# First attention, first block: written order, rows normed a step ahead, row loads on ScalarE's queue

## The chip, the cores and the metric

The kernel runs on one core of a Trainium2 chip. The metric is the device time of one execution in microseconds, as the median of several runs. The engines of the core work side by side, each through its own list of instructions: TensorE (PE in the profile, with PEld for its weight loads) multiplies matrices into PSUM, VectorE (DVE) and ScalarE (ACT) do elementwise work, GpSimd (POOL) does the rest, and SyncE (SP) issues transfers. ScalarE can issue transfers as well.

## The reference

N = 2708 rows of width 256 and an adjacency matrix of N x N go through two layers, each an attention over the graph and a mixture of eight experts. The change lies in the first layer's attention:

```
xn = layernorm(x)                       # per row, no weights
q, k, v = xn @ Wq.T + bq, xn @ Wk.T + bk, xn @ Wv.T + bv
scores = where(adj > 0, q @ k.T / 16, -9e15)
x = x + elu(softmax(scores) @ v)
x = x + experts0(layernorm(x))          # top 2 of 8, gelu
x = x + graph attention of layer 1 (layernorm(x))
x = x + experts1(layernorm(x))
```

## The kernel before

`layer0_attention` handles the queries in six blocks (`BLOCKS`): five of 512 rows and one of 148. For each block it walks over 22 key tiles of 128 rows (`k`, the last has 20 rows). The projections of queries and keys are folded into one matrix `aT`, so that the keys of a tile are simply the normed rows, transposed: `xnT`.

A key step `k` of block `b` does the following. `scores` multiplies `xnT` of the tile with the block's queries `g` (L578), takes the exponential on ScalarE (L590) and multiplies by the mask on VectorE (L593). `attend`, three steps later (`LAG`), multiplies the masked `p` with the values `v` and adds up in four banks of PSUM (L642). In the profile each score step has four matmul records and each attend step eight.

In block 0 the key tiles have to be prepared too, tile `k + 4` in step `k`. `norm_begin` takes statistics on VectorE (L274 to L276) and a power on GpSimd (L280). `norm_end` norms the row tile on VectorE (L284). `prepare` then transposes it on TensorE (`to_columns`, L297), copies the result from PSUM to `xnT` on ScalarE (L298), sums it on VectorE (L491), multiplies it with `wv` on TensorE (L496) and copies the values out on ScalarE (L500). The rows themselves come through `load_x` (L400), nine tiles ahead, into nine buffers (`xin`).

Also in block 0, `masks_of` turns adjacency rows into masks on VectorE (a comparison L438 and a transpose L444): the generator `first_mask` for block 0 and `later_mask` for block 1. Both load through SyncE (L417, four transfers for one buffer) and share three buffers (`adj`).

SyncE issues in written order in the whole kernel. For the other engines a planner orders the instructions by readiness and estimated costs, unless they stand in a region of `manual_schedule`: in such a region each engine that it names issues in the order in which the code emits. Before the change such a region for TensorE, ScalarE and VectorE begins with block 1 and goes on to the end of the first experts; block 0 is the planner's. A smaller region for VectorE and GpSimd covers the norming of tiles 0 to 3 and the first masks. Tiles 0 to 3 are prepared, and the queries of block 0 computed, ahead of the loop.

Of the kernel before, what the change touches and what calls it, by code (L numbers as in the profile page):

```python
# [27 lines left out]
NT = (N + P - 1) // P  # L28
ROWS = [min(P, N - t * P) for t in range(NT)]
# [14 lines left out]
def of_tile(rows, t):  # L44

    if t >= KEYS:
        return rows[t * P : t * P + ROWS[t], :]
    b = t // GROUP * BN
    return rows[b : b + BN, :].rearrange("(p j) d -> j p d", j=GROUP)[t % GROUP]
# [57 lines left out]
def adj_ffn_kernel(ctx: ExitStack, tc: tile.TileContext, a: dict, out: bass.AP):  # L107
    nc = tc.nc
# [267 lines left out]
    def layer0_attention(line):  # L376
        with ExitStack() as scope, ExitStack() as until_last:
# [17 lines left out]
                return pool.tile(shape, dtype, name=f"{name}_last", bufs=bufs)  # L395
            xin = {}

            def load_x(t):
                xin[t] = rows0.tile([P, D], F32, name="xin", bufs=9)
                nc.sync.dma_start(xin[t][: ROWS[t]], of_tile(a["x"], t))  # L400

            def masks_of(b, of):

# [68 lines left out]
            def norm_begin(t):  # L472
                r, src = ROWS[t], xin.pop(t)
                return t, src, norm_stats(src[:r], r)

            def norm_end(t, src, stats):
                r, (mean, factor, *_) = ROWS[t], stats
                xn = rows.tile([P, D], F32, name="xn", bufs=4)
                normed(xn[:r], src[:r], mean, factor)
                return xn  # L480

            def prepare(t, xn):
                r = ROWS[t]
                at = xnT[:, :, t * P : t * P + r]
                if t < NT - 1:
                    to_columns(at, xn[:r], r)
                else:
                    tail_columns(x_tail, xn)
                    nc.vector.tensor_copy(at, x_tail[:, :, :r])
                    r, at = P, x_tail  # L490
                nc.vector.tensor_reduce(  # L491
                    sums_of[:, :, t], xnT[:, :, t * P : t * P + ROWS[t]], AX.X, ALU.add
                )
                ps = misc.tile([P, GROUP, P], F32, name="misc").rearrange("p g n -> p (g n)")
                for c in range(DC):
                    nc.tensor.matmul(  # L496
                        ps[:r, :D], at[:, c, :], wv[:, c, :],
                        start=(c == 0), stop=(c == DC - 1),
                    )
                nc.scalar.copy(v[:r, t, :D], ps[:r, :D])  # L500
# [3 lines left out]
            if True:  # L504
# [8 lines left out]
                with tc.manual_schedule(  # L513
                    engines={mybir.EngineType.DVE, mybir.EngineType.Pool}
                ):
                    begun = [norm_begin(t) for t in range(2)]
# [39 lines left out]
            def queries(b):  # L556
                b0, nb, _ = BLOCKS[b]
                g = of_block(b, "g", [P, DC, nb], F32)
                for d in range(DC):
                    ps = misc.tile([P, GROUP, P], F32, name="misc").rearrange("p g n -> p (g n)")  # L560
                    for c in range(DC):
                        nc.tensor.matmul(
                            ps[:, :nb], aT[:, c, d * P : (d + 1) * P], xnT[:, c, b0 : b0 + nb],
                            start=(c == 0), stop=(c == DC - 1),
                        )
                    nc.scalar.activation(
                        g[:, d, :nb], ps[:, :nb], AF.Identity, bias=cq[:, d : d + 1]
                    )
                return g
# [103 lines left out]
            for t in range(4):  # L673
                prepare(t, first[t])
            g = queries(0)
            late, total, accs, apart = [], None, None, None
            folding = fold_gate(wide)
            for b, (b0, nb, ts_) in enumerate(BLOCKS):
                line.gap = GROUP if b >= last - 1 else GROUP + 1
                if b == 1:  # L680
                    order0.enter_context(
                        tc.manual_schedule(engines={
                            mybir.EngineType.PE,
                            mybir.EngineType.Activation,
                            mybir.EngineType.DVE,
                        })
                    )
                if b + 1 < len(BLOCKS):
                    turned_of[b + 1] = mask_of(b + 1)
                if b == 0:  # L690
                    later_mask = masks_of(1, turned_of)
                    next(later_mask)
                for k in range(NT):
                    if b == 0:
                        if k + 9 < NT:
                            load_x(k + 9)
                        next(first_mask, None)
                        if k + 4 < NT:
                            prepare(k + 4, norm_end(*norm_begin(k + 4)))

                    j = k - (2 if b == last else NT - 1 - GROUP)
                    if 0 <= j < len(ts_):
                        load_x(ts_[j])
                    if k == (0 if b == last else GROUP):
                        apart_adj = load_apart(b)
                    if k == NT - 8:
                        apart = compare_apart(*apart_adj)
                    late.append((b, k, scores(b, k, g, apart, mT)))
                    if len(late) > LAG:
                        b_, k_, p = late.pop(0)  # L710
                        if k_ == 0:
                            accs = [
                                ps_acc.tile([P, D + 1], F32, name="acc") for _ in BLOCKS[b_][2]
                            ]
                        attend(b_, k_, p, accs)
                        if k_ == NT - 1:
                            evict(b_, accs, total)
                    if b == 1 and k % 2 == 0:
                        next(folding, None)
                    if b == 0 and k == NT - 1:  # L720
                        sums = wide.tile([P, DC], F32, name="sums", bufs=1)
                        nc.vector.tensor_reduce(sums, sums_of, AX.X, ALU.add)
                        total = all_sum(wide, sums, wv, D, "total0")
                    if b == 0 and k == NT - 4:
                        raw = wide.tile([P, BN // QUARTER, P], I32, name="adj", bufs=3)
                        raw = raw.rearrange("p n e -> p (n e)").bitcast(F32)
                        nc.sync.dma_start(
                            raw, a["L0_ffn_Wr"].rearrange("d e -> (d e)").partition_broadcast(P)
                        )
                        gate_rows(raw)  # L730
                    if k == NT - 6 and b + 1 < len(BLOCKS):
                        g_next = queries(b + 1)
                    if k % 3 == 2 if b == last - 1 else k == 0 or k >= 2:
                        next(later_mask, None)
                    if k == NT - 3:
                        even_later = iter(())
                        if b + 2 < len(BLOCKS):
                            even_later = masks_of(b + 2, turned_of)
                            next(even_later)
                    if b > 0 and k == 2:  # L740
                        nc.sync.dma_start(neighbours[b - 1][:], turned_of[b - 1])
                    if background and k % 2 == 1 and b < last and (b > 0 or k > 8):
                        background.pop(0)()
                    if b > 0:
                        line.step()
                    if b == last and k == LAG:
                        until_last.close()
                    if b == last and k == LAG + 2:
                        n = FULL_AFTER[experts0.early]
                        guess0 = experts0.open(  # L750
                            [i * (n // RING) * E // (n + GROUP) for i in range(AHEAD)] + [-1]
                        )
                        for _ in range(AHEAD):
                            next(guess0)
                        begin0 = experts0.begin()
                    if b == last and LAG + 2 <= k < LAG + 8:
                        next(begin0)
                    if b == last and k in (LAG + 9, LAG + 13, LAG + 18):
                        next(begin0)
                if b == last:  # L760
                    nc.sync.dma_start(neighbours[b][:], mT)
                else:
                    for _ in later_mask:
                        pass
                    later_mask = even_later
                    g, mT = g_next, turned_of[b + 1]
# [1332 lines left out]
```

## Time and profile before

| what | value |
|---|---|
| median of 3 runs | 1183.81 us (1181.85, 1183.81, 1185.64) |
| profiled execution | 1189.22 us, span of its instructions 1187.4 us |
| granted TensorE clock, mean | 0.985 |
| PE busy | 1128.9 us, 95% of the span |
| DVE busy | 649.2 us, 55% |
| ACT busy | 433.0 us, 36% |
| POOL busy | 410.2 us, 35% |
| moved by DMA | 195.88 MB, mean 165 GB/s |

Busy times are shares of the whole span, while the stages have different limits, so they have to be read stage by stage. A timeline row gives the start in microseconds, the duration, the engine, the line of the code, the operation with its output and inputs, the number of instructions that were merged into the row, and in brackets the idle time of the engine before the row, with what ended it. PE's durations overlap, because matmuls are pipelined; the pace is the distance from start to start.

### The profile page before, as it was taken

Reading aid. Unit: us, or ns where it says so; the run is one execution under the profiler, and the core shown is the slowest. Engines: PE = TensorE matmul, PEld = TensorE weight load, DVE = VectorE, ACT = ScalarE, POOL = GpSimd, SP = SyncE. Lnnn points to the kernel's source line nnn. Section 1 sums busy time; section 2 is a strip of 40 time slices with the busy share of each in tenths; the row PEclk is TensorE's granted clock in tenths of the full one; section 3 lists DMA queues with packets and bytes.
Section 4 is the critical chain, followed back from the end, with each engine's and each line's share of the span. In section 5 each row is a group of like instructions: output and inputs, shape, how many; then the busy total and the mean of one; then the engine's idle time right before and its main releaser. Section 6 shows DMA issues by size and latency. Waiting matters only on the chain. (4 is left out here: it accounts for less than half of the span.)

```text
span 1187.4 us, 20904 instructions
## 1 busy us (share of the span) xinstructions
PE 1128.9 (95%) x6417; PEld 916.1 (77%) x6417; DVE 649.2 (55%) x2401; ACT 433.0 (36%) x1260; POOL 410.2 (35%) x503
## 2 busy tenths in 40 slices
PE   8989999999999999999999999998999998879993
PEld 5665666666666675789999999996999987869992
DVE  5555777787887868552222222223866777512224
ACT  3222222222222222453333333333776758424441
POOL 3001212121212212342433343333645556435542
PEclk9999999999999999999999999999999999989997
DMA  9678677877837567478766935634001527567346
GB/s 218 134 165 207 172 173 180 229 174 200 218 83 188 142 174 267 142 209 248 199 177 189 335 73 158 178 100 107 1 1 45 207 67 222 137 209 230 82 119 237
DMA packets 200006, 195.88 MB, mean 165 GB/s; under 512 B 91004, under 2 KB 182613, under 8 KB 194377
## 3 DMA queue, kind: packets, MB, share of 16 engines
q1 hardware_dynamic: 175546, 123.97, 41.5%
q0 software_dynamic: 23872, 69.76, 18.7%
q8 instruction: 55, 0.90, 0.3%
q14 instruction: 71, 0.57, 0.2%
q10 hardware_dynamic: 462, 0.68, 0.2%
HBM read 246.19 MB, written 66.15 MB: 263 GB/s over the span
## 5 line engine op out<-in xcount | busy, mean ns | idle before, releaser
L1813 PEld LDWEIGHTS mm<-xe,ring 128*128 128x128 f32 x2192 | 262.4, 195 | 24.1 <-DVE xe L1786 8.9
L1813 PE MATMUL mm<-xe,ring 128*128 128x128 f32 x2192 | 265.2, 278 | 15.2 <-DVE xe L1786 7.9
L1821 ACT ACTIVATE hT<-mm,ring 128x128 f32<-128x128 f32 x548 | 155.6, 369 | 269.0 <-issue 177.2
L1829 PE MATMUL acc<-ring,hT 128*128 128x256 f32 x1096 | 252.8, 381 | 0.7 <-issue 0.7
L1829 PEld LDWEIGHTS acc<-ring,hT 128*128 128x128 f32 x1096 | 202.0, 191 | 25.3 <-issue 1.3
L642 PEld LDWEIGHTS acc<-v,p 128*128 128x128 f32 (+1 forms) x880 | 160.0, 190 | 62.4 <-issue 37.4
L642 PE MATMUL acc<-v,p 128*128 128x257 f32 (+1 forms) x880 | 202.7, 383 | 0.0
L578 PE MATMUL s<-g,xnT 128*128 128x512 f32 x420 | 200.3, 597 | 0.6 <-DVE mT L597 0.6
L1835 DVE SCALAR_TENSOR_TENSOR y<-acc,who,bias 128x256 f32<-128x256 f32 x92 | 44.4, 482 | 262.6 <-PE acc L1829 252.6
L1537 POOL DMA_INDIRECT disp<-row,to x88 | 91.6, 1041 | 261.6 <-DVE x L662 123.4
L280 POOL TENSOR_TENSOR ln_rs<-ln_rs,minus_half 128x2 f32<-128x2 f32 x88 | 67.7, 770 | 173.7 <-DVE ln_rs L276 121.1
L922 PE MATMUL acc<-parts,m 128*128 128x266 f32 x924 | 126.2, 293 | 0.0
L1719 POOL DMA_INDIRECT ring<-L_ffn_packed,weight_row x76 | 79.2, 1042 | 125.8 <-PE acc L1829 94.0
L922 PEld LDWEIGHTS acc<-parts,m 128*128 128x128 f32 x924 | 117.0, 185 | 4.1 <-ACT raw L949 0.9
L578 PEld LDWEIGHTS s<-g,xnT 128*128 128x128 f32 x420 | 76.8, 190 | 55.0 <-issue 49.8
L590 ACT ACTIVATE p<-s 128x512 f32<-128x512 f32 x105 | 62.3, 596 | 137.8 <-PE s L578 120.9
L1851 POOL DMA_INDIRECT xd<-y,who x45 | 71.4, 1588 | 111.3 <-DVE xe L1792 49.8
L593 DVE SCALAR_TENSOR_TENSOR p<-p,mT 128x512 f32<-128x512 f32 x100 | 70.9, 709 | 70.5 <-ACT p L590 70.4
L889 ACT CAST m<-mT 128x512 fp32r<-128x512 fp8e4 (+4 forms) x168 | 71.5, 475 | 11.1 <-PE acc L922 6.7
L1841 POOL DMA_INDIRECT xd<-y,who x47 | 50.5, 1075 | 44.5 <-DVE y L1835 34.2
L264 DVE SCALAR_TENSOR_TENSOR row<-x,wr_rows 128x256 f32<-128x256 f32 x128 | 54.3, 425 | 3.3
L1792 DVE TENSOR_SCALAR xe<-xe_raw,ring 128x128 f32<-128x128 f32 x90 | 27.2, 347 | 43.2 <-DMA ring<-L_ffn_packed,weight_row 42.2
(330 smaller groups left out, 1079.7 us busy)
## 6 DMA issues: line engine op xcount, KB each, us to landing
adj<-in_adj_dram SPq DMA_DIRECT2D x100, 256.0 KB
L_ffn_packed<-in_L_ffn_W_dram SPq DMA_DIRECT2D x32, 512.0 KB
xg<-disp SPq DMA_DIRECT2D x368, 32.0 KB
L_ffn_packed<-in_L_ffn_W_dram SPq DMA_DIRECT2D x32, 256.0 KB
neighbours<-mT SPq DMA_DIRECT2D x5, 1408.0 KB
mT<-neighbours SPq DMA_DIRECT2D x5, 1408.0 KB
ring<-L_ffn_packed SPq DMA_DIRECT2D x3, 2182.0 KB
xin<-in_x_dram SPq DMA_DIRECT2D x42, 128.0 KB
```

The costliest lines, as they stand in the source:

```text
L280: nc.gpsimd.tensor_tensor(rs[:r, 1], rs[:r, 0], minus_half[:r], ALU.pow)
L578: nc.tensor.matmul(ps[:kr, :nb], xnT[:, c, k0 : k0 + kr], g[:, c, :nb], start=(c == 0), stop=(c == DC - 1 and k < KEYS),)
L593: nc.vector.scalar_tensor_tensor(p, p, LARGEST, mask, op0=ALU.min, op1=ALU.mult)
L642: nc.tensor.matmul(accs[j][:r], p[keys, q0 : q0 + r], v[keys, k, :], start=(k == 0), stop=(k == NT - 1),)
L889: nc.scalar.copy(m[:, : q1 - q0], MASKS[b].of_key(mTs[b], k)[:, q0 - b * BN : q1 - b * BN],)
L922: nc.tensor.matmul(acc[:r], masks[t], parts[:, k, i], start=(k == 0 and i == 0), stop=False,)
L1537: nc.gpsimd.indirect_dma_start(disp[:], bass.IndirectOffsetOnAxis(ap=to[:r, j : j + 1], axis=0), rows2[:r, j], None,)
L1719: nc.gpsimd.indirect_dma_start(w, None, packed[:], bass.IndirectOffsetOnAxis(ap=self.weight_row[:, s : s + 1], axis=0), bounds_check=E * P ...
L1813: nc.tensor.matmul(ps[:, i, :], w[:, c * hidden + f * P : c * hidden + (f + 1) * P], xe[:, c, :], start=(c == 0), stop=(c == DC - 1),)
L1821: nc.scalar.activation(hT[:, f, :], ps[:, i, :], AF.Gelu, bias=w[:, b1 + f : b1 + f + 1])
L1829: nc.tensor.matmul(ps, hT[:, f, :], w[:, w2 + f * D : w2 + (f + 1) * D], start=(f == 0), stop=(f == hc - 1),)
L1851: start = nc.gpsimd.indirect_dma_start(xd[:], at, y, None, bounds_check=N - 1, oob_is_err=False, compute_op=ALU.add)
```

## The change

Block 0 is now in the region of written order as well: it begins before the loop, with the norming of tiles 4 and 5. The rows of block 0's loop are loaded from ScalarE's queue instead of SyncE's (13 loads, in steps 0 to 12). In step `k` the loop prepares tile `k + 4` from a row that was normed in the step before, norms tile `k + 5`, and begins the statistics of tile `k + 6`.

```diff
-            def load_x(t):
+            def load_x(t, queue=nc.sync):
                 xin[t] = rows0.tile([P, D], F32, name="xin", bufs=9)
-                nc.sync.dma_start(xin[t][: ROWS[t]], of_tile(a["x"], t))
+                queue.dma_start(xin[t][: ROWS[t]], of_tile(a["x"], t))
...
             for t in range(4):
                 prepare(t, first[t])
             g = queries(0)
+            order0.enter_context(
+                tc.manual_schedule(engines={
+                    mybir.EngineType.PE,
+                    mybir.EngineType.Activation,
+                    mybir.EngineType.DVE,
+                })
+            )
+            ahead = [norm_end(*norm_begin(4))]
+            begun = [norm_begin(5)]
...
             for b, (b0, nb, ts_) in enumerate(BLOCKS):
                 line.gap = GROUP if b >= last - 1 else GROUP + 1
-                if b == 1:
-                    order0.enter_context(
-                        tc.manual_schedule(engines={
-                            mybir.EngineType.PE,
-                            mybir.EngineType.Activation,
-                            mybir.EngineType.DVE,
-                        })
-                    )
...
                 for k in range(NT):
                     if b == 0:
                         if k + 9 < NT:
-                            load_x(k + 9)
+                            load_x(k + 9, nc.scalar)
                         next(first_mask, None)
                         if k + 4 < NT:
-                            prepare(k + 4, norm_end(*norm_begin(k + 4)))
+                            prepare(k + 4, ahead.pop(0))
+                        if begun:
+                            ahead.append(norm_end(*begun.pop(0)))
+                        if k + 6 < NT:
+                            begun.append(norm_begin(k + 6))
```

## The prediction

> **What bounds the kernel now.** I read the page, then the busy time by stretches, then the timeline of the first attention's first block.
>
> ```profile
> PE 1128.9 (95%) x6417; PEld 916.1 (77%) x6417; DVE 649.2 (55%) x2401; ACT 433.0 (36%) x1260; POOL 410.2 (35%) x503
> ```
> TensorE is the bound of the whole. Two stretches, the first block and blocks 1 to 4 (us, then busy time of PE, PEld, DVE, ACT, POOL, granted clock, DMA share, GB/s):
>
> ```profile
> 20.36:123.70 103.34, 96.55 (x381) 63.69 (x380) 60.08 (x174) 27.14 (x62) 9.67 (x13) 1.00 0.79 172
> 200.00:450.00 250.00, 250.00 (x1013) 163.18 (x1012) 193.25 (x724) 59.13 (x142) 51.76 (x75) 1.00 0.69 181
> ```
> The block runs from the first transpose of key tile 4 (20.36) to block 1's first scores (123.70). After it TensorE has no gap, so what the block gains or loses arrives undiminished at 450 us. Inside it PE has gaps; the PE timeline shows the rates without a gap, and two of the gaps (start, duration, in brackets the idle time before and its releaser):
>
> ```profile
> 100.27 1.03 PE L496 MATMUL misc<-wv,xnT 128*128 128x256 f32 x4
> 101.13 0.38 PE L297 MATMUL misc<-ident,xn 128*128 128x128 f32 x2
> 101.35 1.02 PE L578 MATMUL s<-g,xnT 128*128 128x512 f32 x2
> 102.21 1.03 PE L496 MATMUL misc<-wv,xnT 128*128 128x256 f32 x4
> ...
> 111.71 0.41 PE L297 MATMUL misc<-ident,xn 128*128 128x128 f32 x2 [0.71 <-DVE ln_mv L275]
> ...
> 123.70 1.98 PE L578 MATMUL s<-g,xnT 128*128 128x512 f32 x4 [0.63 <-DVE mT L597]
> ```
> From start to start: value projection (wv) 0.86, both transposes 0.22, half of one score step 0.86. The planner has put scores between a tile's transposes and its wv, which covers ScalarE's copy in between. Where nothing stands between, the timeline of all engines shows the price, and two long waits for a normed row:
>
> ```profile
> 71.87 0.38 PE L297 MATMUL misc<-ident,xn 128*128 128x128 f32 x2
> 72.29 0.37 ACT L298 COPY xnT<-misc 128x256 f32<-128x256 f32 x1 [6.56 <-PE misc L297]
> ...
> 72.72 1.13 PE L496 MATMUL misc<-wv,xnT 128*128 128x256 f32 x4 [0.46 <-ACT xnT L298]
> ...
> 73.68 0.38 PE L297 MATMUL misc<-ident,xn 128*128 128x128 f32 x2
> ...
> 84.39 0.41 PE L297 MATMUL misc<-ident,xn 128*128 128x128 f32 x2 [2.55 <-DVE ln_rs L276]
> ...
> 95.41 0.41 PE L297 MATMUL misc<-ident,xn 128*128 128x128 f32 x2 [1.03 <-DVE ln_rs L276]
> ```
> 71.87 to 73.68 is 1.81 against 0.22 + 0.86 = 1.08: a bare handoff costs 0.73. The prelude, where tiles 0 to 3 run bare, has 1.87, so 0.79:
>
> ```profile
> 11.32 0.38 PE L297 MATMUL misc<-ident,xn 128*128 128x128 f32 x2
> 12.22 1.13 PE L496 MATMUL misc<-wv,xnT 128*128 128x256 f32 x4 [0.52 <-ACT xnT L298]
> 13.19 0.38 PE L297 MATMUL misc<-ident,xn 128*128 128x128 f32 x2
> ```
> Are the row loads late? SyncE's queue in this block:
>
> ```profile
> 35.94 8.84 SPq L417 DMA_DIRECT2D adj<-in_adj_dram  x8
> 44.82 1.09 SPq L400 DMA_DIRECT2D xin<-in_x_dram  x2
> ...
> 66.39 1.09 SPq L400 DMA_DIRECT2D xin<-in_x_dram  x2
> 67.58 3.10 SPq L417 DMA_DIRECT2D adj<-in_adj_dram  x4
> 70.72 2.03 SPq L400 DMA_DIRECT2D xin<-in_x_dram  x3
> ```
> Rows do stand behind adjacency loads, but the statistics that end in the wait at 84.39 start at 81.45 on VectorE, 10 to 15 us after those issues: VectorE's order is late, not the data.
>
> **What the Trainium skill says.** DMA: Bandwidth & Descriptors, "Issuing engines are not separate DMA queues": issuing from several engines saves only the sequencer's time. No run shows it yet; it fits that I give the queue no gain. Perfetto Trace Analysis, "DMA Instruction — HWDGE (DVE, Sync)": the issuing sequencer is free again only when the descriptors are generated. In the trace ScalarE's four issues at 1177.23 take 1.99 us, 0.50 each. TensorE: Matmul & The Clock Gate, "What's actually happening": the clock drops after an idle window of about 3.4 us. The prelude, with its bare handoffs, shows clock 1.00, so I price none.
>
> **The change part by part.** First the block without gaps: 21 score steps x 1.72 = 36.1; the masks' and the tail's matmuls 0.95 (120.13 to 121.08); 19 attend steps before block 1's scores x 1.73 (125.52 to 127.25) = 32.9; 18 tiles x 1.08 = 19.4; queries of block 1 3.5 (113.69 to 117.22); the sum of values 0.86. Together 93.8 of 103.3: **9.5 us of gaps.** From start to start they are 2.7 + 1.2 + 0.9 of waits for normed rows, 0.8 before block 1, four bare handoffs (59.45, 72.72, 85.26, 96.28) of about 0.73, the rest small.
>
> *Norm ahead, block in written order on DVE: removed 4.8.* Step k now norms row k+5 and begins row k+6, and PE takes row k+4. VectorE's work in a full step: two mask pairs 1.4 (17.22 to 17.92 is one pair), sums 0.33, norming 0.33, statistics 0.8 (8.44 to 9.24), masking p 0.62: 3.5 us in a step of 5.3 (below), so the rows come in time. Its waits in order: POOL's power was begun a step before. The mask of block 1 needs an adjacency load in step 6 whose buffer comes free in step 5; such a load moved data from 36 to 42 and from 43 to 49.5 us, so 6 to 7 us against one step of 5.3. VectorE stands 1 to 2 us there, with the next rows and p queued behind it; p is used three steps later and VectorE regains 1.8 a step, so nothing for PE, 1 to 2 us once if that cover is gone. The reduction for the gate (3.9 us at 119.2) is now fixed in step 18, and is hidden by the same three steps.
>
> *Written order on PE: added 13.5.* prepare() emits transposes, ScalarE's copy, wv; then come scores and attend. On PE nothing stands between, in all 18 tiles; queued behind the waiting wv are this step's scores and attend, and the next transposes. 18 x 0.75 = 13.5 (13.1 at 0.73, 14.2 at 0.79). A step becomes 1.81 + 1.72 + 1.73 = 5.3.
>
> *Written order and loads on ACT: added 3.5.* From step 4 on, the attend (1.73) gives ScalarE time for the exponential (0.2 after the scores, 0.6 long) and the row's issue (0.5) before the next transposes: hidden. In steps 1 to 3 no attend exists yet: the copy starts 0.2 + 0.6 + 0.5 = 1.3 after the transposes instead of 0.47 (11.32 to 11.79), 0.83 late, 2.5 in three. In step 0 ScalarE is still on the queries until 21.31 and then issues: copy at 21.8 instead of 20.83, 1.0. If issues overlap the running activation it is 0.33 x 3 + 0.5 = 1.5. If the first issue waits for an earlier transfer, as SyncE's constants do around 22 to 24 us, it is up to 3 more.
>
> ```profile
> 20.62 0.69 ACT L566 ACTIVATE g<-misc,cq 128x512 f32<-128x512 f32 x1 [1.02 <-PE misc L562]
> ```
> *Loads off SyncE's queue.* 13 issues of about 0.55 leave it; its adjacency loads wait for VectorE's buffers as before. Bytes are the same. 0, either way, for the reason above; the DMA share of 0.79 leaves room.
>
> *End of the block.* The wait of 0.8 stays (0.8 to 1.3): the sum goes VectorE, PE, as before.
>
> Sum: 13.5 + 3.5 + 0.8 = 17.8 of gaps instead of 9.5: **+8.3 us**, block 1 at 132.0. Low end 13.1 + 1.5 + 0.8 - 9.5 = +5.9, high end 14.2 + 6.5 + 1.3 - 9.5 = +12.5. Blocks 1 to 4 are full on PE and give nothing back. The profiled execution took 1189.22 (span 1187.40) and would take about 1197.5; the median of the runs, 1183.81, becomes **1192.1**.
>
> **The rivals.** Around 0.3% (3.6 us) is what can be told from no change.
> - *VectorE becomes the bound*: each wait for adjacency data in order holds rows and p. For it: DMA is busy 0.79; against it: 3.5 of 5.3 us. If three loads hold PE 3 us each: +8.3 + 9 = 1201.
> - *Faster: the handoff gap is covered.* The one place where half the scores stand between (21.62) has a gap of 0.18. If PE had other work there, 18 x 0.18 = 3.2, plus 1.5 and 0.8, is 5.5 against 9.5: -4.0, 1179.8. It decides below (9.5 - 3.5 - 0.8) / 18 = 0.29 per tile. Against it: prepare() as written leaves nothing to put there.
> - *Given back later.* At 468.45 PE comes out of a wait of 1.7 and runs at half speed until 475, so the mean clock of 450 to 500 is 0.90, some 3.5 us. A shift may take this away, with the low end: 5.9 - 3.5 = +2.4, 1186.2.
>
> **Chances.** Forecast 0.62 (1189.7 to 1196.3), VectorE's bound 0.12, covered gap 0.13, given back 0.13. Slower 0.74, same 0.13, faster 0.13. The range 1184 to 1198 holds forecast and given back and leaves out the covered gap and most of VectorE's.
>
> **What would show it.** Right: wv of tiles 4 to 21 each behind about 0.65 of idle PE released by ACT's copy; steps 5.3 us apart; no wait for a normed row; block 1's scores near 132. Wrong: gaps under 0.3, or transposes that wait for VectorE, or block 1 at 132 and the end not later.

## The result and the profile after

The changed kernel takes **1203.55 us** (median of 4 runs, 1202.05 to 1204.52), the kernel before 1184.72 us in the same session: ratio **1.0147**, 95% interval 1.012 to 1.0175 (the two medians alone would give 1.0159). It is slower, as forecast, but by about twice as much, and outside the range. The profiled execution took 1202.86 us, its span 1201.0 us, against a forecast of 1197.5 for such an execution. (The profiled executions differ by 13.6 us and the medians by 18.8. The profile of before happened to be a long one, 1189.22 against a median of 1184.72.)

TensorE's row of the page, and the busy time of the first block, now from 23.42 to 141.00, with the columns as before:

```profile
PE 1132.3 (94%) x6417; PEld 916.8 (76%) x6417; DVE 656.6 (55%) x2401; ACT 434.4 (36%) x1260; POOL 410.0 (34%) x503
```

```profile
23.42:141.00 117.58, 100.70 (x381) 65.67 (x380) 69.41 (x180) 27.71 (x62) 17.53 (x19) 0.97 0.61 137
```

Two things happened. The block begins 3.06 us later (before: 20.36), and it is 14.24 us longer (before: 103.34), so block 1's first scores come 17.3 us later. Nothing of this is given back soon: the first expert matmul starts 17.0 us later (505.57 against 488.59), layer 1 is still 17.0 late at 826.55, and the last experts start 16.4 late (996.46). Only there do the two profiled executions draw nearer: from that point to the end the changed kernel takes 204.5 us and the kernel before 207.3, at mean clocks of 0.95 and 0.94. The medians, 18.8 apart, show nothing given back.

**Inside the block.** PE's timeline of the changed kernel:

```profile
45.71 0.66 PE L297 MATMUL misc<-ident,xn 128*128 128x128 f32 x2 [5.05 <-DVE xn L284]
...
52.59 0.38 PE L297 MATMUL misc<-ident,xn 128*128 128x128 f32 x2
53.43 1.13 PE L496 MATMUL misc<-wv,xnT 128*128 128x256 f32 x4 [0.46 <-ACT xnT L298]
...
57.85 0.38 PE L297 MATMUL misc<-ident,xn 128*128 128x128 f32 x2
...
140.06 1.10 PE L306 MATMUL misc<-wv,spread 128*128 128x256 f32 x4 [2.09 <-DVE spread L303]
141.00 1.88 PE L578 MATMUL s<-g,xnT 128*128 128x512 f32 x4
```

The step from 52.59 to 57.85 is the steady one: 5.26 us, with 0.84 from the transposes to `wv` where 0.22 is their own pace, and 0.97 to the scores at 54.40 instead of 0.86. That is the bare handoff, 0.73, in every tile. In the first four steps ScalarE's copy is later, and the distance is 1.26 (23.42 to 24.68), then three times about 1.11, instead of 0.84. At 45.71 PE has waited for a normed row, some 5.2 us behind the attend before it, and then runs below its pace: this step takes 6.88 instead of 5.26 (from `wv` at 46.83 to the scores 1.87 instead of 0.97). At the end PE waits 2.09 for the sum of values.

Who held the row? VectorE, in its new fixed order, stood behind an adjacency block for block 1's mask, and normed the row only at 45.16. Its timeline, the mask first and then the row:

```profile
43.47 0.43 DVE L438 TENSOR_SCALAR m_rows<-adj 128x512 fp8e4<-128x512 int32 x1 [6.99 <-DMA adj<-in_adj_dram]
...
45.16 0.40 DVE L284 TENSOR_SCALAR xn<-xin,ln_mv,ln_rs 128x256 f32<-128x256 f32 x1
```

And the adjacency block was late because SyncE issued it late. SyncE's queue in the changed kernel, then in the kernel before, where `wg` had gone out at 22.12:

```profile
23.50 0.38 SPq L528 DMA_DIRECT2D wr<-in_L_ffn_Wr_dram  x1
33.62 0.37 SPq L528 DMA_DIRECT2D wg<-in_L_ffn_gate_w_dram  x1
...
34.62 12.57 SPq L417 DMA_DIRECT2D adj<-in_adj_dram  x8
```

```profile
24.80 2.58 SPq L417 DMA_DIRECT2D adj<-in_adj_dram  x4
```

SyncE stood for ten microseconds in front of a small constant, `wg`, which nobody needs yet, with the adjacency rows queued behind it. The view of waits of SyncE's queue (waited in total, times, longest) names what it waited for:

```profile
SPq L528 <- DMA xin<-in_x_dram: 9.7, 1, 9.7
```

It is a row load, and the row loads are on another engine now. The link is a completion counter. In the order of the built program the transfers of SyncE and ScalarE together go through eight such counters, DMAHW0 to DMAHW7, and a transfer waits for the one that used its counter before it. The third of ScalarE's loads and `wg` stand there with the same counter, 1:

```
ACT  L400 DMACopy xin<-in_x_dram 128x256            [waits DMAHW5_49,DMAHW1_49,DVE_49]
SP   L528 DMACopy wg<-in_L_ffn_gate_w_dram 128x2x8  [waits DMAHW1_49]
```

The load raises counter 1 from 48 to 64, and `wg` waits until it stands at 64. The load itself waits in ScalarE's order for a row buffer and for the work of step 2; ScalarE issues it at 31.45, and at 33.62 SyncE goes on. So a load that has left SyncE's queue can still hold that queue.

**Ahead of the block.** All engines of the changed kernel around 8 us:

```profile
7.89 0.39 ACTq L400 DMA_DIRECT2D xin<-in_x_dram  x1
...
8.33 0.65 ACT L537 COPY mT<-misc 128x256 f32<-128x256 f32 x2 [3.16 <-DVE ln_st L274]
...
8.76 1.65 PE L542 MATMUL s<-mT 128*128 128x256 f32 x3 [2.84 <-ACT mT L537]
```

The first of the 13 loads is emitted in step 0. In the built program it stands far ahead of that step in ScalarE's order, between the four copies of the folded matrix `mT`, which belong to the planner's part ahead of the region. Why the planner let it come so early isn't shown. It loads tile 9 into the buffer of tile 0, which is free only when tile 0 is normed (7.41 + 0.45); the bracket of the copies' row names another of VectorE's instructions, but in the built program the load waits for this norm. So ScalarE waits, two copies wait behind it, and the fold's matmuls wait behind those, at 8.76. In the kernel before the same copies and matmuls come 2.6 us earlier, the copies as shown, the matmuls at 6.16:

```profile
5.74 0.80 ACT L537 COPY mT<-misc 128x256 f32<-128x256 f32 x2 [0.35 <-PE misc L536]
```

The block's gaps, against the 93.8 us without any:

| term | forecast | measured | from |
|---|---|---|---|
| bare handoffs, 18 tiles | 13.5 | 13.1 | 18 x 0.73 |
| ScalarE late in steps 0 to 3 | 3.5 | 1.2 | 0.42 + 3 x 0.27 |
| waits for normed rows | 0 | 6.8 | 5.2 + (6.88 - 5.26) |
| end of the block | 0.8 | 2.1 | 140.06 |
| start of the block | 0 | 3.1 | 23.42 - 20.36 |

The measured terms inside the block make 23.2 of 117.58 - 93.8 = 23.8.

### The profile page after: what moved, and what is told of

It is laid out like the page before. It is cut to its first block, busy times and chain, and to the rows that moved or that the text cites. A ratio compares the mean times of both kernels' runs of the same rounds, so it can differ in the third digit from the quotient of the medians.

```text
span 1201.0 us, 20906 instructions
## 1 busy us (share of the span) xinstructions
PE 1132.3 (94%) x6417; PEld 916.8 (76%) x6417; DVE 656.6 (55%) x2401; ACT 434.4 (36%) x1260; POOL 410.0 (34%) x503
## 5 line engine op out<-in xcount | busy, mean ns | idle before, releaser
L438 DVE TENSOR_SCALAR m_rows<-adj 128x512 fp8e4<-128x512 int32 (+1 forms) x105 | 44.2, 421 | 9.3 <-DMA adj<-in_adj_dram 9.2
```

## The experiments

Edits are against the changed kernel unless a line says otherwise. No experiment leaves out any of the computation. Here and below a load of row tile 9 means the first one, in step 0.

**Only the first load back on SyncE's queue** (x9_sync).

```diff
-                            load_x(k + 9, nc.scalar)
+                            load_x(k + 9, nc.sync if k == 0 else nc.scalar)
```

> The changed kernel with only its first ScalarE load (rows of tile 9, step 0) put back on SyncE's queue. Theory (queues): two losses come from where the planner put that load and its followers. It stood ahead of the fold's copies on ScalarE, so that the first transpose of tile 4 came at 23.42 instead of 20.36 us; and SyncE's load of wg waited for the counter of a ScalarE load of step 2, so that block 1's first adjacency came 10 us late and TensorE lost 5.2 us of waiting and 1.6 us of half clock. Without the first load on ScalarE both should go: tile 4 at about 20.4, wg issued before 25, block 1's first scores at about 131 instead of 141.0, time some 10 us under the changed kernel and 7 to 9 above the kernel before. Rival A (prelude alone): 137.9, 3 us under the changed kernel. Rival B (VectorE's written order is what waits, whoever issues): no wait goes, under 1 us.

Measured: 1192.82 us (11 runs), before 1186.73, ratio 1.0059 (1.0039 to 1.0079). One moved transfer out of 13 takes the loss from 14.7 to 5.9 thousandths. The first adjacency transfer for block 1 on SyncE's queue (`wg` went out at 21.24), and block 1's first scores on PE:

```profile
23.84 2.58 SPq L417 DMA_DIRECT2D adj<-in_adj_dram  x4
```

```profile
132.12 3.09 PE L578 MATMUL s<-g,xnT 128*128 128x512 f32 x4
```

Both losses are gone. The block starts at 20.3, SyncE waits for no row load, and PE for no normed row. Twelve loads are still on ScalarE, but the counters fall differently: in the built program `wg` and the four adjacency transfers behind it now stand ahead of all twelve, so none of them waits for one. What is left is the handoffs, ScalarE's late copies in steps 0 to 3 (now 1.9) and the end, a wait of 2.08, after which PE runs at half speed. Of the 1.9, 0.6 are new: in step 1 ScalarE's first load waits for the counter of SyncE's `wr`, and the copy behind it is late. So the counters hold ScalarE as well as SyncE. In cover_x9_gate below, PE's `wv` waits 1.46 at 26.57 behind such a load.

**The loads of steps 1 to 3 on GpSimd, the first left on ScalarE** (rows_10_12_gpsimd), to part the two losses.

```diff
-                            load_x(k + 9, nc.scalar)
+                            load_x(k + 9, nc.gpsimd if 1 <= k <= 3 else nc.scalar)
```

> The changed kernel with the row loads of steps 1 to 3 (tiles 10 to 12) on GpSimd's queue, all others on ScalarE's. Theory (queues): this parts the two losses. The first load stays ahead of the fold's copies, so tile 4's transposes stay at about 23.4; SyncE no longer shares a counter with loads of steps 1 to 3, so wg is issued before 27, the wait of 5.2 us in step 4 and the half clock behind it go, and block 1 begins at about 134.2 instead of 141.0. Rival (the adjacency data is late by itself, DMA being full): wg early, but the wait for block 1's first adjacency stays above 3 us.

Measured: 1202.02 us (4 runs), ratio 1.0114 (1.008 to 1.0147), which can't be told from the changed kernel's by the times. Block 1's scores came at 138.66 and not at 134.2. PE:

```profile
27.51 0.38 PE L297 MATMUL misc<-ident,xn 128*128 128x128 f32 x2
...
138.66 3.14 PE L578 MATMUL s<-g,xnT 128*128 128x512 f32 x4
```

The two parts separate. The late start stays (it is even later, since PE runs at half speed in part of the prelude: `wv` takes 2.08 instead of 1.13 at 17.85), while SyncE's wait for rows shrinks from 9.7 to 0.4, `wg` goes out at 23.99, the adjacency at 26.75, VectorE waits for no adjacency and no normed row is late. So the adjacency was not late by itself. The block from its first transposes to block 1's scores takes 111.2 instead of 117.6. In the traces, then, the first load costs the start, and a later load on ScalarE's queue costs the stall in the block.

**Scores between a tile's transposes and its `wv`** (cover), all loads on ScalarE. `prepare` is split in two, and the step's scores go between the halves.

```diff
-                            prepare(k + 4, ahead.pop(0))
+                            turned = turn(k + 4, ahead.pop(0))
...
+                    if b == 0 and k + 4 < NT:
+                        project(*turned)
```

> The changed kernel with prepare cut in two: in each step of block 0 the transposes and ScalarE's copy, then the scores, then the value projection (wv). Theory (handoff): the idle of about 0.65 and the restart of 0.1 between transposes and wv go in 18 tiles, a full step falls from 5.26 to about 4.5 us, and block 1 begins 11 to 13.5 us earlier than in the changed kernel, at about 128 to 130; time 11 to 13 under the changed kernel, 4 to 7 above the kernel before, since the late start and the late adjacency stay. Rival (VectorE or ScalarE becomes the bound at 4.5 us a step): the steps stay above 4.9 and at most 6 us are gained.

Measured: 1196.02 us (5 runs), ratio 1.0076 (1.005 to 1.0102). Missed: block 1's scores came at 132.41, 8.6 earlier than in the changed kernel and not 11 to 13.5. The view of waits of SyncE's queue, and PE:

```profile
SPq L534 <- DMA xin<-in_x_dram: 13.5, 3, 10.9
```

```profile
46.68 0.66 PE L297 MATMUL misc<-ident,xn 128*128 128x128 f32 x2 [9.05 <-DVE xn L284]
```

No `wv` waits for ScalarE in the loop any more. But SyncE's constants now wait 13.5 us for row loads, the first adjacency transfer goes out at 37.09, and the row is 9.05 late instead of 5.05. The 8.6 gained and the 4.0 lost again make 12.6. With the later start of this block (24.50 against 23.42) and 0.6 more of half speed behind the wait, and without the 1.2 of ScalarE's first steps, 13.1 are left for the handoffs.

**Scores between, and the first load on SyncE** (cover_x9): both edits above.

> The changed kernel with two edits: the first row load back on SyncE's queue, and prepare cut in two so that the scores stand between transposes and wv. In the run with the first load alone put back, block 1 began at 132.1, 1.2 of it at half clock. Theory (handoff): 18 x 0.75 = 13.5 go from there, with the about 1 us by which ScalarE was late in steps 1 to 3; block 1 at 117 to 119, against 123.7 in the kernel before; 4 to 7 us faster than it (ratio 0.994 to 0.997). Rival (VectorE): at steps of 4.5 us its waits for adjacency come through to TensorE; block 1 at 122 or later, no faster than before.

Measured: **1178.44 us** (5 runs), before 1186.53, ratio **0.9928 (0.9896 to 0.996)**. It beats both kernels. PE:

```profile
39.34 0.38 PE L297 MATMUL misc<-ident,xn 128*128 128x128 f32 x2
...
41.28 1.03 PE L502 MATMUL misc<-wv,xnT 128*128 128x256 f32 x4
...
43.88 0.38 PE L297 MATMUL misc<-ident,xn 128*128 128x128 f32 x2
...
118.29 1.88 PE L584 MATMUL s<-g,xnT 128*128 128x512 f32 x4
```

A step is 4.54 instead of 5.26, with no gap in it, and 0.22 + 1.72 + 0.86 + 1.74 is its whole content. Block 1 comes at 118.29, 13.8 before x9_sync, which differs in the split alone. The block starts 0.9 later here (21.22 against 20.28), so it is 14.8 shorter: 13.1 for 18 handoffs of 0.73, 1.9 for ScalarE's late copies and 0.5 for the half speed at the end of x9_sync, less 0.6 of new gaps in the first steps. So the handoffs, forecast at 13.5, come to 13.1 when they are taken away.

**The same, with the gate's reduction behind the sum** (cover_x9_gate): `gate_rows(raw)`, the reduction of step 18, is emitted after the sum of values, for which PE waits 2.08 at the end of the block in cover_x9 too.

> As the kernel with the two edits, and the gate's reduction on VectorE (3.9 us in step 18) moved behind the sum of values at the end of block 0. Theory: the wait of 2.1 us of that sum's matmuls for VectorE falls under 1 us, 1 to 2 us under the kernel with two edits, 6 to 8 under the kernel before. Rival: the reduction then holds the masking of block 1's first steps and TensorE waits there instead; no gain.

Measured: 1178.33 us (6 runs), ratio 0.9925 (0.9897 to 0.9953). The wait is gone and block 1 comes at 116.04, 2.25 earlier, but no gain is measured against cover_x9. The lead is 1.75 at the queries of the next block and is lost around 463 us, where PE waits 1.70 for a normed row in both. Some 0.9 us after the wait's end the four records of an attend on PE take 1.99 in this kernel, first fence, and 1.14 in cover_x9, second:

```profile
462.12 1.99 PE L648 MATMUL acc<-v,p_last 128*128 128x257 f32 x4
```

```profile
463.88 1.14 PE L648 MATMUL acc<-v,p_last 128*128 128x257 f32 x4
```

**TensorE left to the planner in block 0**, ScalarE and VectorE in written order, with all loads on ScalarE (pe_planned) and with the first on SyncE (pe_planned_x9).

```diff
                 tc.manual_schedule(engines={
-                    mybir.EngineType.PE,
                     mybir.EngineType.Activation,
                     mybir.EngineType.DVE,
                 })
...
+                if b == 1:
+                    order0.enter_context(
+                        tc.manual_schedule(engines={mybir.EngineType.PE})
+                    )
```

> The changed kernel with TensorE left to the planner in block 0 (written order for ScalarE and VectorE from before the loop, for TensorE from block 1 on). Theory (handoff): the planner puts scores or attends between transposes and wv where it can, so most of the 13.5 us go, as in the kernel before; 8 to 13 us under the changed kernel. Rival (what costs is the order of VectorE and ScalarE, not TensorE's): under 4 us are gained.

> The changed kernel with the first row load back on SyncE's queue and TensorE left to the planner in block 0. It tells what the order on TensorE is worth once the queue's losses are gone. Theory (only the cover of the handoff matters, whoever provides it): block 1 at 117 to 121, within 3 us of the kernel that has the scores between transposes and wv in written order (118.3). Rival (the planner's own placing costs more than the handoff): block 1 at 123 or later, no faster than the kernel before.

Measured: 1196.3 us (7 runs), ratio 1.0072 (1.005 to 1.0093), and 1182.64 us (16 runs), before 1187.69, ratio 0.996 (0.9944 to 0.9976). In the first, PE waits 5.32 for a normed row at 50.00. In the second that is gone; three bare handoffs remain, PE waits 1.39 for a mask at 120.00, and block 1's first scores come in two halves, at 120.00, within the theory, and at 122.27, between it and the rival. With norming ahead and ScalarE and VectorE in written order, the planner covers most handoffs by itself. Its median is 4.2 us above that of the order written with scores between (cover_x9), but the intervals of the two ratios overlap. In the profiles it is 3.1 behind at the attend that follows block 1's first scores (123.13 against 120.01).

**One part of the change alone, on the kernel before.** Only the loads on ScalarE (queue_only: `load_x(k + 9, nc.scalar)`, order left to the planner), and only the norming ahead (ahead_only: the `ahead` and `begun` lists, loads on SyncE, planner).

> The kernel before with nothing but the 13 row loads of block 0 moved to ScalarE's queue; the order stays the planner's. Theory (the data was not what TensorE waited for): within 3 us of the kernel before, and slower rather than faster if the planner puts a load ahead of the fold's copies or a load holds a counter that SyncE needs. Rival (late loads were the cause of the waits at 84 and 95 us): at least 4 us faster.

> The kernel before with nothing but the rows normed a step ahead in the code (tile k + 5 normed and k + 6 begun in step k); loads on SyncE's queue, order the planner's until block 1. Theory: part of the 4.8 us of waits for normed rows goes, 1 to 5 us faster. Rival (the planner orders by its own estimates and sets the rows where it did): within 1 us of the kernel before.

Measured against 1186.53: 1195.52 us (5 runs), ratio 1.0092 (1.0055 to 1.0129), and 1194.42 us (9 runs), ratio 1.006 (1.0036 to 1.0083). Both are slower. For queue_only the size was missed: the planner put many of the loads early into ScalarE's order, SyncE then waited 19.2 us in all for row loads in the first 45 us, and the adjacency left at 41.86 instead of 24.80:

```profile
41.86 2.58 SPq L417 DMA_DIRECT2D adj<-in_adj_dram  x4
```

The block starts 4.4 us later (24.79), and at 96.08 PE waits 1.99 for a masked `p`. The rest of the 9 us wasn't followed up.

For ahead_only the sign was missed. Emitting the norms earlier doesn't make the planner run them earlier. PE waits for normed rows 2.55, 1.03 and 0.71 as in the kernel before, and 2.56 once more, and behind the two long waits it now runs at half speed (`wv` in 2.08 below, where 1.13 is usual):

```profile
61.54 0.41 PE L297 MATMUL misc<-ident,xn 128*128 128x128 f32 x2 [2.56 <-DVE ln_rs L276]
62.42 2.08 PE L496 MATMUL misc<-wv,xnT 128*128 128x256 f32 x4 [0.46 <-ACT xnT L298]
```

**Scores between, all loads on GpSimd** (cover_gpsimd: as cover, with `load_x(k + 9, nc.gpsimd)`).

> The changed kernel with prepare cut in two and all 13 row loads on GpSimd's queue, so that none stands on ScalarE and none shares SyncE's counters. Theory: ScalarE's queue does nothing for the time but harm through the first load; block 1 at 117 to 120 as with the first load on SyncE, 4 to 7 us faster than the kernel before. Rival: the power of the norm on GpSimd waits behind the loads' issues, rows come late and TensorE waits for them; block 1 at 122 or later.

Measured: 1188.1 us (12 runs), before 1187.69, ratio 1.0018 (1.0001 to 1.0036); block 1 at 123.46. GpSimd holds neither SyncE's constants nor ScalarE's copies (in the built program its transfers use other counters), and the start is early (19.77). The number is the rival's, the cause is not. PE waits for no power of GpSimd's, but twice for rows behind late adjacency; VectorE's timeline shows the longer one:

```profile
36.15 0.43 DVE L438 TENSOR_SCALAR m_rows<-adj 128x512 fp8e4<-128x512 int32 x1 [5.40 <-DMA adj<-in_adj_dram]
```

Five row loads go out between 8.23 and 13.19 here, ahead of need, and the adjacency transfers that follow land later. VectorE gets this adjacency 3.6 later than in cover_x9 (36.15 against 32.53), and 3.2 of that are in SyncE's own issue already (27.28 against 24.04). That the five early loads cause the later issue wasn't tested.

## Why the prediction was right and wrong

*The direction* was right, and so was its main reason. Written order lays all 18 handoffs bare: the steady step is 5.26 (forecast 5.3), and the handoffs come to 13.1 (forecast 13.5), bare in the changed kernel and taken away in cover_x9. The waits for late normed rows of the kernel before are gone, as "Norm ahead" said. VectorE has room: outside the one stall, steps run at 5.26 with no row late. What the block loses arrives almost undiminished: 17.0 of 17.3 us at 505 and at 826.

*The step that failed is "Loads off SyncE's queue", priced at "0, either way".* It priced bytes and issue time. The page DMA: Bandwidth & Descriptors of the Trainium skill, "Issuing engines are not separate DMA queues", says that other issuing engines save only sequencer time, and the run that moved the loads alone (queue_only, ratio 1.0092) shows no gain. But no gain was read as no cost. The cost came twice, 3.1 at the start and 6.8 in the block, and both by order and waits. A load that waits for its buffer stops everything behind it on the engine it is moved to. And through a shared completion counter it also stopped the queue that it was moved from. VectorE, said to stand 1 to 2 us for adjacency in step 6, stood 6.99 at the first of block 1's masks, which the code emits in step 2, and the row behind it, for step 4, was late. The text had the danger in sight on one side only, as up to 3 us on ScalarE "if the first issue waits for an earlier transfer", and didn't ask what would wait for the loads. x9_sync shows the size: with the first load back, both losses go, and block 1 comes at 132.12, where the forecast put 132.0. That agreement is partly luck: in x9_sync ScalarE's term is 1.6 smaller than forecast and the end of the block, with its half speed, 1.8 larger.

*"Written order and loads on ACT"*, 3.5, was too much; inside the block it measured 1.2. The alternative named there is what happens, an issue overlaps the running exponential. ScalarE's timeline:

```profile
27.57 0.60 ACT L590 ACTIVATE p<-s 128x512 f32<-128x512 f32 x1 [1.34 <-PE s L578]
27.65 0.34 ACTq L400 DMA_DIRECT2D xin<-in_x_dram  x1
```

*"End of the block"*, 0.8 to 1.3, was too little; it measured 2.1. The gate's reduction, fixed in step 18 on VectorE, was said to be hidden by three steps' lead. It is for `p`, but not for the sum of values that follows it. cover_x9_gate shows this: moved behind the sum, the wait is gone.

*The clock*, of which it said "so I price none", was right for the handoffs: the granted clock is 1.00 from 60 to 145 us, with one in every tile. But the wait of 5.2 us, which the forecast did not have, brought half speed with it, and that step lost 1.6.

*The rivals.* "VectorE becomes the bound" was nearest in number (1201), and its mechanism is half there. Adjacency in VectorE's fixed order held a row, once and not three times; the cause was SyncE's late issue, not VectorE's load or the DMA's (its share in the block fell from 0.79 to 0.61). "The handoff gap is covered" didn't occur in the change, but is real once other work is put there: with the first load on SyncE it gives 1178.44. "Given back later" was not seen: the lag is 17.0 at 505 us, behind the wait that this rival named.

## What to carry to other kernels

Before moving a transfer to another engine's queue, ask what that transfer waits for, what stands behind it there, and which transfers of other queues share its completion counter. In written order, look at each producer and consumer on PE across another engine: with nothing between them every tile pays the handoff (0.73 us here), and a score step of 1.72 us put between hides all of it. A price of nothing needs two reasons, one for no gain and one for no cost.

## What the runs showed of the hardware

TensorE's half speed was met after single waits much shorter than the forecast reckoned with, and not reliably. After waits of 2.56 and 2.55 (ahead_only) and of 1.70 (cover_x9_gate) PE ran at half speed; after 2.55 in the kernel before (84.39) and the same 1.70 in cover_x9 it didn't. At the end of the block a wait of 2.07 or 2.08 was followed by half speed in x9_sync, rows_10_12_gpsimd and cover_gpsimd, and one of 2.08 or 2.09 was not in cover, cover_x9 and the changed kernel. The Trainium skill, TensorE: Matmul & The Clock Gate, "What's actually happening", names an idle window of about 3.4 us; these waits are below it, so the measurements differ from a reading in which one wait must fill the window. What decides in a given execution stays open; no run was made for it. It cost 1.6 us in the changed kernel and some 2.5 in cover_x9_gate, and in the two executions profiled that is where the lead of 1.75 goes.
